# Reordering the opening of a small-attention block: blank products, spare buffers, work moved to GpSimd, loads one a turn

## The chip, the cores and the metric

The kernel runs on one core of a Trainium2 chip. The metric is the device time of one execution in microseconds, as the median of several runs. A core has TensorE (PE in the profile; PEld is its weight load), VectorE (DVE), ScalarE (ACT), GpSimd (POOL) and SyncE (SP, which here only issues DMA transfers). Each engine works through its own list of instructions in order and waits on semaphores for the others.

## What is computed

The reference takes x, 64 sequences of 32 tokens with 256 features in f32, a context of 64 x 257 tokens of 256 features, and a mask. It adds residual blocks, each on a layer norm of x without weights: (1) cross-attention, 16 heads of 16 features, on the first 32 context tokens with a causal window and rotary positions; (2) causal self-attention of the same shape with rotary positions on even and odd features; (3) a linear layer with fp8-quantised weights and activations; (4) cross-attention on all 257 context tokens; (5) a gated mixer with a cumulative sum and a short convolution; (6) a mixture of eight experts, two per token, with one shared. Only the opening of blocks 1 and 2 is touched by the change. Cut to that:

```python
y = (x - mean(x)) / sqrt(var(x) + 1e-5)
q = rope(y @ Wq.T + bq) * d**-0.5        # 16 heads of d = 16
k = rope(ctx[:, :32] @ Wk.T + bk)        # block 2: from y
v = ctx[:, :32] @ Wv.T + bv              # block 2: from y
p = softmax(where(causal, q @ k.T, -inf))
x = x + (p @ v) @ Wo.T + bo
```

## The kernel before

The 2048 tokens stand in SBUF as four tiles `xs[g]` of 512 tokens (128 partitions x 4 x 256). `small_attentions` (L246 to L628) computes blocks 1 and 2 as eight groups n = 0 to 7: n = 0 to 3 are the four token tiles in block 1, n = 4 to 7 the same in block 2. A group has four **turns** t of 128 tokens, called (n,t) below. The Python loops fix the order: every instruction issued through the wrappers (L106 for DVE, ACT, POOL and SP, L118 for products, L121 for transposes) is kept in program order on its engine. So an instruction that waits holds all that follows it on its engine, SP's transfers included.

In turn (n,t) five stages of different tiles run side by side (`line`): the scores of tile t, the sums and the exponentials' transpose of earlier tiles, the context product, the change to feature order, the output product and its addition to x. Beside them the turn prepares group n+1: `rotated` makes one of four rotations (keys c = 0 and 1, then queries c = 0 and 1, in turns 0 to 3), `values` makes v and stores it to DRAM (`v_rows`), `blocks` loads v back in block form (`vb`, whose other places are zeros from a clear at the start), and `spread_keys` copies the keys into block form (`kb`). The layer norm of group n+2 (`norm_steps`, L123 to L182) is a generator stepped by `prepare`: its pieces are the statistics, then mean, variance and three Newton passes for the inverse root, then y in two halves. `opened` transposes y (psT, then ACT copies it to yT).

A rotation is: TensorE product into PSUM (`ps_qk`), DVE's `part` = (product + bias) x sine, four DMA copies `far` that swap blocks of 32 partitions, `near` = (product + bias) x cosine (on DVE for group 0, on ACT and POOL for the others), and the addition near + far on POOL into kT or qT. `near`, `part` and `far` come from rings of two, two and three buffers: a third `near` waits until the first has been added.

The first group's preparation stands ahead of the loop (L500 to L538). The loads are issued by the generator `first_loads` (L632 to L661), stepped by `next(loads)`: before the loop three times, and at the end of turns while n < 3 (in turn 0 the keys' source `kvT` of group n+2 is loaded instead). `raw` (128 x 512 bytes) holds the fp8 weights of block 3; DVE reads it (CAST scratch<-raw) as the first piece of a list of side jobs, in turn (1,0).

Of the kernel before, what the change touches and what calls it, by code (L numbers as in the profile page):

```python
# [7 lines left out]
F32 = mybir.dt.float32  # L8
BF16 = mybir.dt.bfloat16
# [55 lines left out]
def perceiver_kernel(ctx: ExitStack, tc: tile.TileContext, a: dict, out: bass.AP):  # L65
# [54 lines left out]
    def turn(ps, src, eye):  # L120
        return kept(nc.tensor.transpose(ps, src, eye))  # L121

    def norm_steps(g, eng=None, apart=False, ts=range(NT), by_act=False):  # L123

        x = xs[g]
        n, t0 = len(ts), ts[0]
        st = small.tile([P, n, 6], F32, tag="st", name="st")
        mv = small.tile([P, n, 2], F32, tag="mv", name="mv")
        for t in range(n):
            vector.bn_stats(st[:, t, :], x[:, t0 + t, :])  # L130
        if apart:
            yield
        for t in range(n):
            vector.bn_aggr(mv[:, t, :], st[:, t, :])

        ve = small.tile([P, n], F32, tag="ve", name="ve")
        vector.tensor_scalar(ve, mv[:, :, 1], EPS, None, ALU.add)
        half = small.tile([P, n], I32, tag="half", name="half")
        vector.tensor_scalar(half, ve.bitcast(I32), 1, None, ALU.logical_shift_right)
        r0 = small.tile([P, n], I32, tag="r0", name="r0")  # L140
        vector.tensor_scalar(r0, half, -1.0, float(0x5F3759DF), ALU.mult, ALU.add)
        r = r0.bitcast(F32)
        for _ in range(3):
            sq = small.tile([P, n], F32, tag="sq", name="sq", bufs=6)
            rn = small.tile([P, n], F32, tag="rn", name="rn", bufs=6)
            if eng is vector:
                vector.tensor_tensor(sq, r, r, ALU.mult)
                vector.scalar_tensor_tensor(sq, sq, -0.5, ve, ALU.mult, ALU.mult)
                vector.scalar_tensor_tensor(rn, sq, 1.5, r, ALU.add, ALU.mult)
            else:  # L150
                gpsimd.tensor_tensor(sq, r, r, ALU.mult)
                gpsimd.tensor_tensor(sq, sq, ve, ALU.mult)
                gpsimd.tensor_scalar(sq, sq, -0.5, 1.5, ALU.mult, ALU.add)
                gpsimd.tensor_tensor(rn, sq, r, ALU.mult)
            r = rn
        if by_act:
            off = small.tile([P, n], F32, tag="off", name="off")
            gpsimd.tensor_scalar(off, mv[:, :, 0], -1.0, 1.0, ALU.mult, ALU.mult)
            gpsimd.tensor_tensor(off, off, r, ALU.mult)
        yield  # L160
        y = ypool.tile([P, n, D], F32, tag="y", name="y")
        for t in range(n):
            if by_act:
                scalar.activation(
                    y[:, t, :],
                    x[:, t0 + t, :],
                    AF.Identity,
                    bias=off[:, t : t + 1],
                    scale=r[:, t : t + 1],
                )  # L170
            else:
                vector.tensor_scalar(
                    y[:, t, :],
                    x[:, t0 + t, :],
                    mv[:, t, 0:1],
                    r[:, t : t + 1],
                    ALU.subtract,
                    ALU.mult,
                )
            if t == 1 and n > 2:  # L180
                yield
        return y  # L182
# [63 lines left out]
    def small_attentions(layers, first_loads, decode, sides, load_layer1, layer1):  # L246
# [27 lines left out]
            scalar.copy(mk, cst[:, at : at + S][:, None, :].to_broadcast([P, 8, S]))  # L274
            masks.append(mk)

        def clear(vb, engine):
            engine.memset(vb.rearrange("p b h g e -> p (b h g e)"), 0.0)

        def fetch(n):  # L280
            layer, g = order[n]
# [22 lines left out]
        def rotated(it, i, c):  # L304

            src, cs, sn = (
                (it["kvT"], cos, sin) if i == 1 else (it["yT"], cosq, sinq)
            )
            place = "kT" if i == 1 else "qT"
            if c == 0:  # L310
                it[place] = kT_all if i == 1 else qT_([P, 2, GT], "qT")
            dst = it[place]
            w, v0 = it["w"], it["v0"]
            ps = pa([P, GT], "ps_qk")
            proj(ps, lambda k: w[:, i, k, c * P : (c + 1) * P], lambda k: src[:, k, :])

            def by_place(table):
                return table.rearrange("p (o q) -> p o q", o=1).to_broadcast([P, 16, S])

            def by_seq(tile_):  # L320
                return tile_.rearrange("p (b q) -> p b q", q=S)

            bias = vec[:, v0 + 2 * i + c : v0 + 2 * i + c + 1]
            part = part_([P, GT], "part")
            vector.scalar_tensor_tensor(
                by_seq(part), by_seq(ps), bias, by_place(sn), ALU.add, ALU.mult
            )

            far = far_([P, GT], "far")
            for at in range(0, P, S):  # L330
                queue = scalar if (it["n"], i, c) == (0, 0, 1) and at >= 2 * S else sync
                queue.dma_start(out=far[at : at + S, :], in_=part[at ^ S : (at ^ S) + S, :])
            near = near_([P, GT], "near")
            if it["n"] > 0:
                scalar.activation(near, ps, AF.Identity, bias=bias)
                gpsimd.tensor_tensor(by_seq(near), by_seq(near), by_place(cs), ALU.mult)
            else:
                vector.scalar_tensor_tensor(
                    by_seq(near), by_seq(ps), bias, by_place(cs), ALU.add, ALU.mult
                )  # L340
            return lambda: gpsimd.tensor_tensor(dst[:, c, :], near, far, ALU.add)
# [156 lines left out]

        kT_all = sb.tile([P, 2, GT], F32, tag=wide[4], name="kT")
        eye = sb.tile([P, S], BF16, tag="eye", name="eye")  # L500
        loads = first_loads()
        next(loads)
        it = group(0, fetch(0))
        next(loads)
        after = group(1, fetch(1))
        next(loads)
        for half in range(2):
            clear(vbs[0][half], vector)
            clear(vbs[1][half], gpsimd)
        scalar.copy(ident_bf, ident)  # L510
        mask(0)
        it["y"] = finish(norm_steps(order[0][1], vector))
        it["kb"] = [None, None]
        adds = [rotated(it, 1, 0)]
        opened(it)
        mask(1)
        vector.tensor_tensor(eye, ident[:, 0:S], ident[:, 64 : 64 + S], ALU.add)
        steps = norm_steps(order[1][1], vector, apart=True)
        next(steps)
        adds.append(rotated(it, 1, 1))  # L520
        adds[0]()
        for part in range(2):
            spread_keys(it, 0, 0, part)
        adds.append(rotated(it, 0, 0))
        adds.append(rotated(it, 0, 1))
        adds[1]()
        for part in range(2):
            spread_keys(it, 0, 1, part)
# [1 line left out]
            add()  # L530
        for pair in range(2):
            values(it, pair)
        after["y"] = finish(steps)
        for half in range(2):
            blocks(it, half)
        now = it


        line = [None] * 5
        adds = []  # L540
# [1 line left out]
        for n in range(len(order) + 1):  # L542
# [3 lines left out]
                after["kb"] = [None, None]  # L546
            kvT = coming = None
            if n + 2 <= last:
                side = norm_steps(order[n + 2][1], None if n else vector, apart=True)
            else:  # L550
                side = sides

            def prepare(at):
                if n + 2 <= last and at:
                    try:
                        next(side)
                    except StopIteration as end:
                        return end.value

            for t in range(NT):  # L560
                if line[2]:
# [5 lines left out]
                    elif after is not None:  # L567
                        kb_now = (after, 0, t - 2)
                due, adds = adds, []
                if t == 0:  # L570
                    for add in due:
                        add()
                    due = []
# [4 lines left out]
                if after is None:  # L578
                    next(layer1, None)
                else:  # L580
                    y = prepare(t % 2 == 1)
                    adds.append(rotated(after, *((1, 0), (1, 1), (0, 0), (0, 1))[t]))
                if line[3]:
                    by_feature(line[3])
                prepare(t % 2 == 0)
                if n + 2 > last:
                    next(side, None)
                    next(side, None)
# [9 lines left out]
                    next(layer1, None)  # L598
                elif t % 2 == 0:
                    values(after, t // 2)  # L600
                    if (n, t) == (0, 0):
                        opened(after)
                elif t == 3:
                    for half in range(2):
                        blocks(after, half)
                    if n + 2 <= last:
                        coming = group(n + 2, kvT)
                        coming["y"] = y
                        opened(coming)
                line[0] = scores(now, t) if n <= last else None  # L610
                if (n, t) == (last, NT - 1):
                    pair_pool.close()
# [19 lines left out]
    def first_loads():  # L632
# [12 lines left out]
        sync.dma_start(out=xs[1], in_=x_view[1])  # L645
        yield
        sync.dma_start(out=xs[2], in_=x_view[2])
        sync.dma_start(out=w_cur[:, 3], in_=a["w_l0x"][:, 3])
        row_load(R_XO0)
        sync.dma_start(out=xs[3], in_=x_view[3])  # L650
        yield
        sync.dma_start(out=raw, in_=a["w_fp8"])
        for at in (R_AO0, R_FF, R_XO1, R_GO):
            yield
            row_load(at)
        for i in range(0, 4, 2):
# [1382 lines left out]
```

## Time and profile before

| | us |
|---|---|
| median of 3 runs (lowest, highest) | 921.27 (919.26, 922.29) |
| the profiled execution, time | 918.21 |
| its span in the profile | 916.4 |
| PE busy in the span | 853.7 (93%) |
| DVE, POOL, ACT busy | 590.7, 498.1, 424.3 |
| first product of group 0 starts | 7.53 |
| first norm's y complete (DVE) | 10.48 |
| first addition of keys kT (POOL) | 17.86 |
| last addition of queries qT ends (POOL) | 26.08 |
| first scores, (0,0) | 30.24 |
| first scores of (0,1), (0,2), (0,3) | 32.84, 37.56, 44.09 |
| first scores of (1,0), (1,1) | 50.48, 55.14 |

A timeline line is: start, busy time, engine, program line, operation, output<-inputs, shapes, count, and in brackets the idle time of the engine just before and what ended it. Times are in microseconds from the start of the span. L106, L118 and L121 are the wrappers, so a line is found by its tile's name. PE is the product, PEld its weight load beside it. Since POOL and DVE are timed by records of the same profile, rows of one can be set beside the other's by their start times.

### The profile page before, as it was taken

To read this page: it belongs to the slowest core of one execution; us is meant where nothing else is said; L and a number is where in the kernel's file an instruction comes from. 1 tells how busy PE (TensorE), PEld (TensorE's weight loads), DVE (VectorE), ACT (ScalarE), POOL (GpSimd) and SP (SyncE) were. 2 spreads that over 40 slices of the span, in tenths; PEclk is the share of its full clock that TensorE was granted. 3 is DMA by queue.
4 is the path that set the end of the run, shared out by engine and by line. 5 is a ranking of instruction groups with operands and counts; after the bars stand their busy time and mean duration, and the time that the engine had idled before them with its cause. 6 is when DMAs were issued, how large, how long until landed. Compare 5 with 4: busy or idle time off the path is not lost. (4 is left out here: it accounts for less than half of the span.)

```text
span 916.4 us, 22803 instructions
## 1 busy us (share of the span) xinstructions
PE 853.7 (93%) x8699; PEld 587.5 (64%) x8699; DVE 590.7 (64%) x1729; ACT 424.3 (46%) x1100; POOL 498.1 (54%) x982
## 2 busy tenths in 40 slices
PE   6899999989899999999999999998989879999993
PEld 3466666665456666666666666565656648888882
DVE  7888777896677578676777566878655862111117
ACT  2566666653655454554554556654443212222210
POOL 3577777764865566474755566746542124555430
PEclk9999999989999999999999999999799979999997
DMA  7445333453011001111111013000001046777758
GB/s 245 140 135 142 97 90 102 126 154 94 24 53 53 28 28 53 53 54 53 53 53 41 14 53 99 2 2 24 1 25 35 24 155 202 235 231 227 220 181 275
DMA packets 66926, 88.79 MB, mean 97 GB/s; under 512 B 32480, under 2 KB 50688, under 8 KB 64768
## 3 DMA queue, kind: packets, MB, share of 16 engines
q1 hardware_dynamic: 63264, 77.75, 28.2%
q0 software_dynamic: 3456, 9.44, 3.1%
q8 instruction: 69, 1.13, 0.5%
q14 instruction: 41, 0.34, 0.1%
q10 hardware_dynamic: 96, 0.13, 0.1%
HBM read 65.80 MB, written 13.11 MB: 86 GB/s over the span
## 5 line engine op out<-in xcount | busy, mean ns | idle before, releaser
L106 ACT ACTIVATE e<-e,xnm 128x257 f32<-128x257 f32 x256 | 127.2, 499 | 51.2 <-DVE xnm L106 45.7
L106 DVE CUSTOM_DVE_ANT_0 e<-ps_s,mask 128x257 f32<-128x257 f32 x256 | 93.5, 421 | 49.8 <-PE ps_s L118 49.4
L118 PE MATMUL ps_k<-ct,w_w_l1x 128*128 128x512 f32 x256 | 122.3, 600 | 1.6 <-ACT yT L106 0.6
L118 PE MATMUL ps_v<-w_w_l1x,ct 128*128 128x256 f32 x512 | 121.9, 381 | 0.0
L106 POOL TENSOR_SCALAR e<-e,xsm 128x256 f32<-128x256 f32 x256 | 121.3, 492 | 0.0
L121 PE MATMUL ps_t<-cst,e 128*128 128x128 f32 x640 | 102.7, 283 | 7.8 <-DVE eT L106 6.8
L106 DVE COPY eT<-ps_t 128x512 f32<-128x512 f32 x128 | 88.0, 687 | 28.5 <-PE ps_t L121 28.1
L118 PEld LDWEIGHTS ps_v<-w_w_l1x,ct 128*128 128x128 f32 x512 | 94.1, 192 | 11.1 <-issue 0.2
L106 POOL TENSOR_TENSOR x<-x,rows 128x256 f32<-128x256 f32 x96 | 70.8, 753 | 41.9 <-ACT y L106 16.9
L106 ACT ACTIVATE kT<-ps_k,vec 128x512 f32<-128x512 f32 x64 | 44.0, 688 | 100.7 <-PE ps_k L118 100.4
L121 PEld LDWEIGHTS ps_t<-cst,e 128*128 128x128 f32 x640 | 71.9, 142 | 26.3 <-DVE eT L106 7.6
L106 ACT ACTIVATE hTr<-ps_h,w 128x256 f32<-128x256 f32 (+1 forms) x80 | 31.3, 450 | 115.3 <-issue 88.9
L106 DVE TENSOR_TENSOR og<-ps_o,b 128x512 f32<-128x512 f32 (+1 forms) x20 | 12.8, 638 | 104.5 <-PE ps_o L118 104.5
L118 PEld LDWEIGHTS ps_k<-ct,w_w_l1x 128*128 128x128 f32 x256 | 44.5, 190 | 41.3 <-issue 35.3
L1802 POOL DMA_INDIRECT r_rows<-og,lv x36 | 35.5, 986 | 61.3 <-DVE og L106 56.4
L118 PE MATMUL ps_h<-ygT,w 128*128 128x256 f32 (+1 forms) x320 | 65.8, 359 | 0.6 <-issue 0.6
L118 PE MATMUL ps_o<-w,hTr 128*128 128x256 f32 x288 | 65.3, 379 | 0.0
L106 ACT COPY v<-ps_v 128x512 f32<-128x512 f32 x80 | 46.4, 581 | 38.6 <-PE ps_v L118 38.5
L106 POOL TENSOR_TENSOR last<-e,xsm 128x4 f32<-128x4 f32 x64 | 12.9, 202 | 88.9 <-DVE xsm L106 88.9
L118 PEld LDWEIGHTS ps_h<-ygT,w 128*128 128x128 f32 x320 | 54.9, 190 | 6.6 <-issue 0.8
L118 PEld LDWEIGHTS ps_o<-w,hTr 128*128 128x128 f32 x288 | 54.4, 190 | 7.2
L106 ACT ACTIVATE kb<-kT,cst 128x256 f32<-128x256 f32 x96 | 45.4, 512 | 27.2 <-POOL kT L106 25.4
(207 smaller groups left out, 1655.9 us busy)
## 6 DMA issues: line engine op xcount, KB each, us to landing
ct<-in_ctxT SPq DMA_DIRECT2D x16, 1024.0 KB
w<-in_ew SPq DMA_DIRECT2D x20, 514.0 KB
w<-in_ew SPq DMA_DIRECT2D x20, 512.0 KB
far<-part SPq DMA_DIRECT2D x126, 64.0 KB
v_rows<-v SPq DMA_DIRECT2D x16, 256.0 KB
vb<-v_rows SPq DMA_DIRECT2D x64, 64.0 KB
r<-r_rows SPq DMA_DIRECT2D x8, 512.0 KB
b<-in_eb SPq DMA_DIRECT2D x20, 128.0 KB
```

What stands on the lines that cost most here:

```text
L106: ins = getattr(self.engine, name)(*args, **kw)
L118: return kept(nc.tensor.matmul(ps, **args))
L121: return kept(nc.tensor.transpose(ps, src, eye))
L1802: wrote = nc.gpsimd.indirect_dma_start(out=r_rows, out_offset=bass.IndirectOffsetOnAxis(ap=write_i[:, at : at + 1], axis=0), in_=o[:, i, : ...
```

## The change

In the order of the diff:

1. `norm_steps` can stop once more (`split`) ahead of the Newton passes. Group 1's norm uses it: statistics, mean and variance stand before the keys' additions, the Newton passes after the queries' products.
2. All four clears of `vb` (128 x 2048 f32 each) are on GpSimd; before, two were on DVE.
3. Both rotations of group 0's keys are issued ahead of the transposes of y.
4. Their `part` and `near` take buffers of the scores' rings (tags sc0, sc1, e0, e1), which hold nothing until the first scores; the queries' come from the two rings as before.
5. DVE clears a bf16 tile `blank`, and TensorE multiplies it by itself 14 times (128x512 each) into PSUM bank b5 ahead of all else. Nothing reads the result.
6. Group 2's norm: its Newton passes run on GpSimd instead of DVE, and its pieces move: statistics in turn (0,1), mean, variance and Newton passes in (0,2), all of y in (0,3). Before, the four pieces came one a turn from (0,0) to (0,3).
7. In all turns of group 0 the additions near + far left by the turn before come first; before, they came first in turn 0 only, and in the others after the feature-order stage.
8. `opened` of group 1 moves from the end of turn (0,0) to that of (0,1). Group 0's eight block loads move from before the loop into turns (0,0) and (0,1), four each.
9. `first_loads` has one more stop: x2 is issued once the values of group 0 are made, w_l0x[3] and a rows load in turn (0,1), x3 in (0,2), raw and another rows load in (0,3), and the rest a turn or more later than before. Before, x2, w_l0x[3], rows and x3 were issued at the start and raw in (0,1).

```diff
-    def norm_steps(g, eng=None, apart=False, ts=range(NT), by_act=False):
+    def norm_steps(g, eng=None, apart=False, ts=range(NT), by_act=False, split=False):
...
         r = r0.bitcast(F32)
+        if split:
+            yield
         for _ in range(3):
...
-        def clear(vb, engine):
-            engine.memset(vb.rearrange("p b h g e -> p (b h g e)"), 0.0)
+        def clear(vb):
+            gpsimd.memset(vb.rearrange("p b h g e -> p (b h g e)"), 0.0)
...
-            part = part_([P, GT], "part")
+            spare = (it["n"], i) == (0, 1)
+            part = sb.tile([P, GT], F32, tag=f"sc{c}", name="part") if spare else part_([P, GT], "part")
...
-            near = near_([P, GT], "near")
+            near = sb.tile([P, GT], F32, tag=f"e{c}", name="near") if spare else near_([P, GT], "near")
...
+        blank = sb.tile([P, GT], BF16, tag="e2", name="blank")
+        vector.memset(blank, 0.0)
+        idle = psum.tile([P, GT], F32, tag="b5", name="idle")
+        for _ in range(14):
+            mm(idle, lhsT=blank[:, 0:P], rhs=blank, start=True, stop=True)
         loads = first_loads()
         next(loads)
         it = group(0, fetch(0))
         next(loads)
         after = group(1, fetch(1))
-        next(loads)
-        for half in range(2):
-            clear(vbs[0][half], vector)
-            clear(vbs[1][half], gpsimd)
+        for vb in vbs[0] + vbs[1]:
+            clear(vb)
...
-        adds = [rotated(it, 1, 0)]
+        adds = [rotated(it, 1, c) for c in range(2)]
         opened(it)
...
-        steps = norm_steps(order[1][1], vector, apart=True)
+        steps = norm_steps(order[1][1], vector, apart=True, split=True)
         next(steps)
-        adds.append(rotated(it, 1, 1))
+        next(steps)
         adds[0]()
         for part in range(2):
             spread_keys(it, 0, 0, part)
         adds.append(rotated(it, 0, 0))
         adds.append(rotated(it, 0, 1))
+        next(steps)
         adds[1]()
...
         for pair in range(2):
             values(it, pair)
+        next(loads)
         after["y"] = finish(steps)
-        for half in range(2):
-            blocks(it, half)
...
-                side = norm_steps(order[n + 2][1], None if n else vector, apart=True)
+                side = norm_steps(order[n + 2][1], apart=True)
...
+            ahead, behind = ((0, 1, 0, 1), (1, 0, 1, 0)) if n else ((0, 0, 1, 2), (0, 1, 0, 0))
...
-                if t == 0:
+                if t == 0 or n == 0:
                     for add in due:
                         add()
...
-                    y = prepare(t % 2 == 1)
+                    y = prepare(ahead[t])
...
-                prepare(t % 2 == 0)
+                prepare(behind[t])
...
-                    if (n, t) == (0, 0):
-                        opened(after)
+                elif (n, t) == (0, 1):
+                    opened(after)
...
+                if n == 0 and t < 2:
+                    blocks(now, t)
                 line[0] = scores(now, t) if n <= last else None
...
         sync.dma_start(out=xs[2], in_=x_view[2])
+        yield
         sync.dma_start(out=w_cur[:, 3], in_=a["w_l0x"][:, 3])
         row_load(R_XO0)
+        yield
         sync.dma_start(out=xs[3], in_=x_view[3])
         yield
         sync.dma_start(out=raw, in_=a["w_fp8"])
-        for at in (R_AO0, R_FF, R_XO1, R_GO):
+        row_load(R_AO0)
+        for at in (R_FF, R_XO1, R_GO):
             yield
             row_load(at)
```

More of the change, by code (lines that the diff above doesn't have):

```diff
@@ L548, in small_attentions, with prepare @@
             if n + 2 <= last:
-                side = norm_steps(order[n + 2][1], None if n else vector, apart=True)
+                side = norm_steps(order[n + 2][1], apart=True)
             else:
                 side = sides
-            def prepare(at):
-                if n + 2 <= last and at:
+            def prepare(count):
+                y = None
+                for _ in range(count if n + 2 <= last else 0):
                     try:
@@ L557, in prepare @@
                     except StopIteration as end:
-                        return end.value
+                        y = end.value
+                return y
+            ahead, behind = ((0, 1, 0, 1), (1, 0, 1, 0)) if n else ((0, 0, 1, 2), (0, 1, 0, 0))
             for t in range(NT):
```

## The prediction

> **What bounds the kernel now.** I read the table of busy time in ten-microsecond windows first, then the timelines of the engines from 7 to 58 us (the change ends where the second group begins), then the issues on SP's queue. In the windows the columns are engine busy time (PE, PEld, DVE, ACT, POOL), the granted clock, the DMA share and GB/s:
>
> ```profile
> 0.00:10.00 10.00, 2.47 (x3) 1.17 (x4) 7.94 (x25) 1.89 (x3) 3.73 (x6) 1.00 0.78 269
> 10.00:20.00 10.00, 8.89 (x30) 4.73 (x28) 6.31 (x14) 2.22 (x6) 2.04 (x3) 1.00 0.77 250
> 20.00:30.00 10.00, 6.86 (x27) 4.36 (x28) 9.14 (x27) 4.22 (x11) 4.69 (x6) 1.00 0.52 141
> 30.00:40.00 10.00, 9.69 (x180) 5.99 (x179) 8.46 (x28) 5.91 (x13) 4.44 (x5) 1.00 0.52 149
> 40.00:50.00 10.00, 9.06 (x107) 5.82 (x106) 8.35 (x18) 8.14 (x18) 7.45 (x8) 1.00 0.43 116
> 50.00:60.00 10.00, 9.35 (x173) 6.11 (x172) 9.03 (x24) 6.48 (x16) 6.10 (x17) 1.00 0.66 183
> 60.00:70.00 10.00, 10.00 (x184) 7.34 (x183) 7.89 (x15) 6.55 (x16) 7.91 (x10) 1.00 0.34 95
> ```
>
> From 60 us on TensorE has no idle time. What the opening gains or loses for TensorE by then stays to the end; there are some 14 us of idle TensorE before 60 us, 7.5 of them before the first product. From 50 us on DVE has no gap either, and its order is fixed by the program:
>
> ```profile
> 48.64 0.75 DVE L106 SCALAR_TENSOR_TENSOR part<-ps_qk,vec,cst 128x512 f32<-128x512 f32 x1 [0.77 <-PE ps_qk L118]
> 49.31 1.39 DVE L106 BATCH_NORM_STATS2 st<-x 128x6 f32<-128x256 f32 x4
> 50.62 1.22 DVE L106 CAST scratch<-raw 128x512 int32<-128x512 int8 x1
> 51.77 0.68 DVE L106 TENSOR_REDUCE mx<-pair_bank 128x16 f32<-128x512 f32 x1
> ```
>
> The cast at 50.62 starts with nothing ahead of it to wait for, because its load was issued at 38.53 and landed at 42.30. Everything behind it runs back to back until 57.6 at least.
>
> **The opening, part by part.** (Turn (n,t) is turn t of group n; part and far are the rotation's product and its partition-swapped copy.)
>
> Clears. DVE loses two clears of 1.77 us, the second ending at 5.14; the statistics of x0 (5.06) then start when x0 is there (4.65), so the first norm ends at 10.17 instead of 10.48. GpSimd gets four at 1.80: 0.73 to about 7.9, so the clears stand beside the small Newton operations that begin at 6.7. What a clear does to a DVE operation on two SBUF inputs no row shows: DVE's and GpSimd's clears overlap without slowing (1.77 and 1.80), and against a GpSimd addition DVE's small operations are blocked for as long as the addition lasts:
>
> ```profile
> 23.65 1.23 DVE L106 SCALAR_TENSOR_TENSOR rn<-sq,rn 128x4 f32<-128x4 f32 x1
> 24.91 1.19 DVE L106 TENSOR_TENSOR sq<-rn 128x4 f32<-128x4 f32 x1
> ```
>
> (0.16 alone.) So the price lies between 0 and one clear's rest, 1.2 to 1.4: y of x0 ends between 10.2 and 11.5. I take half. [...]
>
> Blank products. The first key product took 3.37 us, the second 1.95; the granted clock reads 1.00 at both, so that column doesn't show what made the first slow. One blank costs between 0.27 (a bf16 128x256 row, warm) and 0.84 (a quarter of the 3.37, which is four records): 14 of them 3.8 to 11.8 us, in idle time until 7.5. I take 0.27 x 1.73 = 0.47 each, 6.5, ending at 8.0. Then k0 is ready at 8.0 + 1.95 = 9.95, hidden by y's end in place of 10.94. If they don't warm anything, k0 is at 11.4 and k1 at 14.7; if each takes 0.84, they end at 13 and the opening loses 2: the two ends. [...]
>
> Keys first, spare buffers. Before, part k0 is at 10.94 and part k1 at 14.49 (behind transposes), the near of q0 waits for the kT addition (19.16) and that of q1 too (20.98). After, k0 at 10.2 and k1 at about 11.5; the queries no longer wait for the ring. A rotation costs 0.75 for part, 2.42 to issue its four copies, 1.4 to land. With the bulk loads out of the way, kT0 is added at 15.0 (17.86), kT1 at 17.5 (19.68), the queries' copies land at 21.2 (24.20) and the last query addition ends at 22.6 (26.09). With the block of 1.3 each is 1.3 later. So the first scores come at 23.6 to 25, against 30.24. The second norm's Newton is issued after the queries' products; it is free of their near waits but meets the additions, at one blocked operation (1.2) each. The first key product of group 1 (before: 28.08) starts its rotation at 22.9 to 25.9; I take 25.0, **3.1 earlier**.
>
> **The turns of group 0.** Here that gain is spent. Group 2's norm (x2) ran on DVE: 33.46 to 35.2 for Newton. Now it runs on GpSimd, as x3's does in before: 12 operations from 55.64 to 58.93, 3.3 us, issued behind the addition of kT11, which waits for far11. TensorE's transposes of y stand before scores (0,3), so they wait for it. From the start of the first rotation of group 1: part 0.75, copies 2.5, one v_rows store 0.45, four block loads now moved into turn 0 at 0.49 = 1.95, the kvT load 0.45, copies of far11 2.5, landing 1.45: 10.05. Then kT11 1.27, the spread 0.5, Newton 3.3, y 1.4: 16.5; with 0.25 of hand-overs 16.75. DVE's y is delayed by up to two GpSimd additions that follow (near and qT): 0, 1.25 or 2.5. So q1's part of group 1 starts 16.75 to 19.25 after the first; before:
>
> ```profile
> 28.08 0.75 DVE L106 SCALAR_TENSOR_TENSOR part<-ps_qk,vec,cst 128x512 f32<-128x512 f32 x1
> ...
> 42.31 1.25 DVE L106 TENSOR_SCALAR y<-x,mv,rn 128x256 f32<-128x256 f32 x2
> 43.48 0.74 DVE L106 SCALAR_TENSOR_TENSOR part<-ps_qk,vec,cst 128x512 f32<-128x512 f32 x1
> ```
>
> 15.4 after. With 25.0 + 18.2 = 43.2 the gain is **0.3 us** of 3.1 (ends: 22.9 + 16.75 = 39.7, a gain of 3.8, and 25.9 + 19.25 = 45.2, a loss of 1.7). TensorE, given the first scores five us earlier, waits in turn (0,3) instead. Sums first costs nothing: the additions that it moves ahead are waited for by the keys' spread behind them anyway. x2, w3, rows and x3 land late but ahead of use: x2 is wanted at about 30, and is issued at about 22.
>
> **The raw load.** It moves from the end of turn (0,1) to the end of (0,3). On SP it then stands behind the last rotation's copies and the eight block loads:
>
> ```profile
> 42.88 0.49 SPq L106 DMA_DIRECT2D rows<-in_rows  x1
> 44.29 2.42 SPq L106 DMA_DIRECT2D far<-part  x4
> 46.75 4.86 SPq L106 DMA_DIRECT2D vb<-v_rows  x8
> 51.66 0.45 SPq L106 DMA_DIRECT2D rows<-in_rows  x1
> ```
>
> Its place is that of the last line: 51.66 less 0.3. From the end of the q1 part: copies 2.45, blocks 3.9 (at 0.49) to 4.86, own issue 0.5 to 0.6, landing 1.45 (a far copy) to 3.2 (this load before; the rows load above took 2.73, to 54.84): 8.3 to 11.1. The cast comes 6.4 after that end. DVE stalls **1.9 to 4.7, I take the middle, 3.3**, and nothing takes that up: mx of (1,0), which stands behind the cast, waits, then the part of group 2's first query, then the chain to ACT's cT, for which TensorE waits already:
>
> ```profile
> 57.71 1.13 PE L118 MATMUL ps_p<-w_w_l0x,cT 128*128 128x256 f32 x4 [0.65 <-ACT cT L106]
> ```
>
> **Sum.** -0.3 + 3.3 = 3.0 us later for TensorE at 60 us, and so at the end. The profiled execution took 918.21 us (span 916.4 and 1.8 around it), so it would take 921.2; the median of the runs, 921.27, stands 3.06 above that execution, so I forecast **924.3**. The ends: a gain of 3.8 with a stall of 1.9 gives -1.9, 919.4; a loss of 1.7 with 4.7 gives +6.4, 927.7.
>
> **Rivals.**
> - *The opening's gain reaches the end (faster).* Place: the x2 chain. If far11 isn't held by SP's queue (the block loads issued in the shade of other waits) and GpSimd's Newton is done before y is wanted, scores (0,3) come when TensorE's own work allows: from first scores at 24 and the 13.85 between (0,0) and (0,3) in before, 37.9 against 44.09, 6.2 earlier. With the smaller stall, 1.9, that leaves 4.3: 917.0. It decides from the point at which the q1 part comes before 40. For it: 14 us of idle TensorE to take. Against: the sum of 16.75, each term from a row.
> - *Gain and stall cancel.* The raw load lands like a far copy (stall 1.9) and the opening keeps some 2 us: 921.3. For: the load is 64 KB (128x512 of one byte), no more than one far copy. Against: it took 3.19 in before.
> - [...] Clears block the first norm (1.3), GpSimd's additions block y twice (2.5): q1 part at 45.2, stall 4, +5.7: 927.0. For: the rows of 1.23 and 1.19. Against: before had such blocks in the second norm too.
> - *The blanks don't warm.* Then k1 comes at 14.7 as before, 1.3 more: inside the forecast's range.
>
> **How the numbers follow.** Forecast 0.55 (own range 919.4 to 927.7), gain reaches the end 0.24, cancel 0.09, lock twice 0.12. About 0.3% (2.76 us) is what a measurement of this kernel can tell from no change. Of the forecast's 0.55 some 0.36 lies above +2.76 and 0.19 within it. So slower 0.36 + 0.12 = 0.48, same 0.19 + 0.09 = 0.28, faster 0.24. The range takes in half of the first rival below and the lock's end above: 916.5 to 928.5.
>
> **What would show it.** First scores at 23.6 to 25; Newton of x1 with one or two entries of 1.2; the first key part of group 1 at 23 to 26; GpSimd's x2 Newton directly behind kT11; the psT of group 2 waiting for y; the raw load on SP behind the eight block loads, and ahead of the cast an idle time of 2 to 5 us put down to the DMA of raw. It would be wrong if the q1 part came before 40, or the cast did not wait, or if TensorE had idle time after 60 us that took up a delay.

## The result and the profile after

The changed kernel takes **925.57 us** (median of 8 runs, 924.02 to 928.49); the kernel before took 920.88 beside it (8 runs, 918.99 to 922.29). The ratio is 1.0058, interval 1.0043 to 1.0074: slower by 4.0 to 6.8 us. Its profiled execution took 925.07 us, span 923.3 (before: 918.21 and 916.4).

Windows of the changed kernel (columns as in the prediction):

```profile
0.00:10.00 10.00, 8.04 (x19) 3.00 (x20) 5.25 (x21) 1.89 (x3) 7.22 (x8) 1.00 0.78 265
...
20.00:30.00 10.00, 9.68 (x115) 6.08 (x113) 9.52 (x21) 6.55 (x15) 4.74 (x5) 1.00 0.58 170
30.00:40.00 10.00, 7.55 (x95) 4.53 (x94) 6.80 (x17) 6.30 (x13) 5.44 (x9) 1.00 0.71 183
40.00:50.00 10.00, 5.50 (x89) 4.13 (x90) 6.07 (x9) 3.47 (x8) 5.83 (x12) 0.66 0.49 143
```

TensorE works 2.8 us more from 20 to 30 us than before, and 5.7 us less from 30 to 50 us. Of its 8.04 us in the first ten, 5.96 go to the blank products, which nobody reads.

The opening did what it was meant to do: the first scores start at 24.69 us instead of 30.24. Half of the lead is gone at the third tile, and all of it at the fourth. First scores of each turn, from the timelines of TensorE:

| turn | before | after | difference |
|---|---|---|---|
| (0,0) | 30.24 | 24.69 | -5.55 |
| (0,1) | 32.84 | 28.70 | -4.14 |
| (0,2) | 37.56 | 35.01 | -2.55 |
| (0,3) | 44.09 | 46.63 | +2.54 |
| (1,0) | 50.48 | 53.53 | +3.05 |
| (1,1) | 55.14 | 58.92 | +3.78 |
| (1,2) | 62.44 | 67.43 | +4.99 |
| (2,0) | 74.36 | 79.36 | +5.00 |

Two places turn the lead into a loss: ahead of (0,3), where 5.1 us go, and between (1,0) and (1,2), where 1.9 go. From there to (2,0) the difference stays at 5.0. Of the 3.0 us lost from (0,0) to (0,2), 1.4 come with the transposes of group 1's y, which the change moved behind the first scores, and 1.33 are a wait for yT at 31.37.

**The first place.** GpSimd of the changed kernel, from the addition of the second keys' rotation of group 1:

```profile
37.21 1.27 POOL L106 TENSOR_TENSOR kT<-near,far 128x512 f32<-128x512 f32 x1 [3.99 <-DMA far<-part]
38.46 0.48 POOL L106 TENSOR_SCALAR kb<-kT,cst 128x256 f32<-128x256 f32 x1
38.90 0.21 POOL L106 TENSOR_TENSOR sq<-r 128x4 f32<-128x4 f32 x1
...
41.99 0.20 POOL L106 TENSOR_TENSOR rn<-sq,rn 128x4 f32<-128x4 f32 x1
42.14 1.26 POOL L106 TENSOR_TENSOR near<-near,cst 128x512 f32<-128x512 f32 x1
43.48 1.26 POOL L106 TENSOR_TENSOR qT<-near,far 128x512 f32<-128x512 f32 x1
```

and DVE, which waits for the last Newton operation and then stands through GpSimd's two large operations:

```profile
42.23 3.48 DVE L106 TENSOR_SCALAR y<-x,mv,rn 128x256 f32<-128x256 f32 x4 [3.71 <-POOL rn L106]
45.62 0.74 DVE L106 SCALAR_TENSOR_TENSOR part<-ps_qk,vec,cst 128x512 f32<-128x512 f32 x1
```

Undisturbed, the four operations of y take 1.38 (a row of the kernel before, from group 1's norm):

```profile
26.79 1.38 DVE L106 TENSOR_SCALAR y<-x,mv,rn 128x256 f32<-128x256 f32 x4
```

Here they take 3.48. TensorE meanwhile:

```profile
38.50 0.38 PE L121 MATMUL ps_c<-cst,o 128*128 128x128 f32 x2
43.70 0.44 PE L121 MATMUL psT<-cst,y 128*128 128x128 f32 x1 [4.82 <-DVE y L106]
44.95 1.76 PE L121 MATMUL psT<-cst,y 128*128 128x128 f32 x7 [0.81 <-DVE y L106]
46.63 0.41 PE L118 MATMUL pair_bank<-mk,eye 64*32 64x256 bf16 x8
46.82 1.08 PE L118 MATMUL pair_bank<-kb,qT 64*32 64x128 f32 x32
```

and in the kernel before:

```profile
43.39 0.78 PE L121 MATMUL psT<-cst,y 128*128 128x128 f32 x4 [0.94 <-DVE y L106]
44.09 0.30 PE L118 MATMUL pair_bank<-mk,eye 64*32 64x256 bf16 x8
44.22 0.64 PE L118 MATMUL pair_bank<-kb,qT 64*32 64x128 f32 x32
```

A second cost stands behind the wait of 4.82. The granted clock, 0.66 as the mean of the ten microseconds, is 1.00 until 40.97, 0.50 from there to 47.79 (the last 2.7 of the wait and the work behind it) and 1.00 again from then on; at 0.50 the 32 score products take 1.08 instead of 0.64.

**The second place.** SP's queue, and DVE at the cast:

```profile
46.42 2.41 SPq L106 DMA_DIRECT2D far<-part  x4
48.90 5.39 SPq L106 DMA_DIRECT2D vb<-v_rows  x8
54.33 0.45 SPq L106 DMA_DIRECT2D raw<-in_w_fp  x1
```

```profile
52.36 1.40 DVE L106 BATCH_NORM_STATS2 st<-x 128x6 f32<-128x256 f32 x4
56.41 0.43 DVE L106 CAST scratch<-raw 128x512 int32<-128x512 int8 x1 [2.65 <-DMA raw<-in_w_fp]
56.76 0.68 DVE L106 TENSOR_REDUCE mx<-pair_bank 128x16 f32<-128x512 f32 x1
```

The raw load stands behind the block loads, the cast waits 2.65 us for it, and everything behind the cast waits with it. TensorE meets this as a wait for cT, 1.66 long; before, the same wait was 0.65, at 57.71:

```profile
62.71 1.13 PE L118 MATMUL ps_p<-w_w_l0x,cT 128*128 128x256 f32 x4 [1.66 <-ACT cT L106]
```

### The profile page after: what moved, and what is told of

Read it like the earlier page. It is cut to its first block, busy times and chain, and to the rows that moved or that the text cites. A ratio compares the mean times of both kernels' runs of the same rounds, so it can differ in the third digit from the quotient of the medians.

```text
span 923.3 us, 22828 instructions
## 1 busy us (share of the span) xinstructions
PE 858.3 (93%) x8713; PEld 588.8 (64%) x8713; DVE 588.7 (64%) x1719; ACT 424.5 (46%) x1100; POOL 503.4 (55%) x996
## 5 line engine op out<-in xcount | busy, mean ns | idle before, releaser
L106 POOL TENSOR_TENSOR x<-x,rows 128x256 f32<-128x256 f32 x96 | 70.7, 752 | 45.2 <-ACT y L106 19.0
L106 POOL DMA_INDIRECT yg<-y_rows,lv x36 | 35.1, 975 | 39.7 <-DVE lv L106 29.1
```

Of the source, the lines that this page charges most:

```text
L106: ins = getattr(self.engine, name)(*args, **kw)
```

## The experiments

The theory: the cost is those two places, the Newton passes on GpSimd and the late raw load; the other parts gain or do nothing. The main rivals: one of the two is hidden behind the other; or the opening's gain is lost in group 0 whatever is done. In the table, "first scores (2,0)" is from each kernel's profile, against 74.36 in the kernel before; ratios are to the kernel before.

| kernel | median us | before beside it | ratio (95%) | first scores (2,0) |
|---|---|---|---|---|
| changed | 925.57 | 920.88 | 1.0058 (1.0043 to 1.0074) | +5.00 |
| raw early | 924.68 | 920.69 | 1.0044 (1.0029 to 1.0058) | +4.33 |
| norm 2 put back | 927.67 | 920.69 | 1.0075 (1.0058 to 1.0092) | +8.19 |
| both | 922.77 | 920.69 | 1.0021 (1.0009 to 1.0033) | +2.52 |
| before, raw late | 924.07 | 920.69 | 1.0029 (1.0017 to 1.0042) | +3.92 |
| norm 2's Newton on DVE | 922.15 | 920.63 | 1.0007 (0.9992 to 1.0022) | +2.49 |
| two clears on DVE | 925.67 | 920.63 | 1.0056 (1.0040 to 1.0072) | +6.19 |
| no blank products | 926.20 | 920.63 | 1.0060 (1.0038 to 1.0082) | +4.81 |
| three parts undone | 919.59 | 920.63 | 0.9981 (0.9966 to 0.9996) | -0.94 |
| the same, y in halves | 920.68 | 920.61 | 0.9996 (0.9980 to 1.0013) | -0.73 |
| before, opening alone | 919.46 | 920.61 | 0.9982 (0.9970 to 0.9994) | -1.29 |
| the same, with blanks | 918.58 | 919.95 | 0.9981 (0.9966 to 0.9996) | -1.72 |
| the same, with the turns | 918.74 | 919.95 | 0.9981 (0.9967 to 0.9995) | -1.65 |

The last column and the medians go together to about 1.2 us: the time is decided by then.

**Raw early.**

```diff
         sync.dma_start(out=xs[2], in_=x_view[2])
+        sync.dma_start(out=raw, in_=a["w_fp8"])
         yield
...
-        sync.dma_start(out=raw, in_=a["w_fp8"])
         row_load(R_AO0)
```

> The changed kernel, with the load of raw issued directly behind x2's (about 23 us) instead of at the end of turn (0,3). In the changed kernel the cast waits 2.65 us for it (56.41) and TensorE meets that again in a wait of 1.66 us for cT at 62.71. Theory (two separate losses, the late norm of group 2 and the late raw load): the cast starts at about 53.8, the output product at 62.71 comes 2.2 earlier, and the time falls from 925.6 to 923.3. Rival (the late norm alone sets the end, the cast's wait stands beside it): no idle time ahead of the cast, but 925.6 as before.

The cast has no idle time any more (54.68, right behind the statistics); the time falls by 0.9, not 2.3, and the intervals of the two ratios overlap. In the profiled execution the first query products took 5.40 us instead of 3.70, so first scores came 1.7 later for a reason that is not in the edit; but that execution, 922.54, was the fastest of the six, so this does not explain the median. Between (1,0) and (1,2) this kernel takes 12.23, the changed one 13.90, the kernel before 11.96: the second place is closed. By the medians alone the theory's size isn't shown here.

**Norm 2 put back, alone and with raw early.**

```diff
-                side = norm_steps(order[n + 2][1], apart=True)
+                side = norm_steps(order[n + 2][1], None if n else vector, apart=True)
...
-            ahead, behind = ((0, 1, 0, 1), (1, 0, 1, 0)) if n else ((0, 0, 1, 2), (0, 1, 0, 0))
+            ahead, behind = (0, 1, 0, 1), (1, 0, 1, 0)
```

> The changed kernel, with group 2's norm as in the kernel before: Newton passes on DVE, one piece a turn from (0,0) to (0,3). Theory: TensorE's wait of 4.82 us for y ahead of scores (0,3) goes, scores (0,3) come at 40 to 42 instead of 46.63 and TensorE is 4 to 5 us earlier from there; the raw load still stands behind the eight block loads, so the cast still waits 2 to 4 us: 920.5 to 921.5. Rival (the chain is that of the rotations' copies and additions, not the norm): scores (0,3) within 1 us of 46.6 and 925.

> The changed kernel with both edits: raw issued behind x2's load, and group 2's norm as in the kernel before. Theory (the two losses add up, and the opening's gain is real): 925.6 - 2.2 - 4.5 = 918.9, some 2 us below the kernel before (920.9), with the cast not waiting and scores (0,3) at 40 to 42. Rival (the opening's gain is taken away by something else, the block loads or the sums first): 920.9 or above.

Alone it gains nothing (927.67 against 925.57, with intervals that overlap), and the expectation failed: scores (0,3) came at 46.93. With both edits the 918.9 that was expected failed too, and 922.77 is the rival's side. The wait for y at (0,3) is gone, but another has come ahead of it. TensorE with both edits:

```profile
30.30 0.66 PE L121 MATMUL ps_t<-cst,e 128*128 128x128 f32 x4
36.90 3.75 PE L118 MATMUL ps_qk<-yT,w_w_l0x 128*128 128x512 f32 x4 [5.94 <-ACT yT L106]
```

In the kernel before, Newton ran on DVE in turn (0,1), ahead of the rotation of that turn, while the transposes of group 1 were already done. The change has moved those transposes into (0,1): ACT's yT copies stand behind the near of that turn's rotation (34.41), which waits for DVE's part (33.56), which stands behind Newton. The four query products behind the wait take 3.75 us instead of 1.88; the granted clock is 0.68 as the mean of 30 to 40 us, and 1.00 there in the kernel before. So the place of the norm's pieces had to change with the transposes; the engine was free, as the run with Newton on DVE below shows. With the norm put back, the raw load counts in full: the two kernels differ in that load alone, and by 4.9 us.

**Before, raw late.**

```diff
-        sync.dma_start(out=raw, in_=a["w_fp8"])
         for at in (R_AO0, R_FF, R_XO1, R_GO):
             yield
+            if at == R_FF:
+                sync.dma_start(out=raw, in_=a["w_fp8"])
             row_load(at)
```

> The kernel before, with one edit: the load of raw issued at the end of turn (0,3), where the changed kernel has it (behind the eight block loads), all else as it was. Theory (the late load alone costs its wait): issue at about 51.7, landing 53.7 to 54.5, so the cast waits 2.3 to 3.2 us, less the 0.8 by which it is shorter when no GpSimd operation blocks it: 922.5 to 923.5 against 920.9. Rival (TensorE has enough queued work to hide it): 920.9.

The load is issued at 53.08 behind 5.66 us of block loads, the cast waits 4.00, and the kernel before becomes 3.4 us slower (2.7 by the ratio, interval 1.6 to 3.9). One late 64 KB load is enough. In its profile 0.64 of the 3.92 us at (2,0) stand already at (1,0), ahead of the cast, so some 3.3 are the load's. The rival falls: TensorE had no queued work to hide it.

**Norm 2's Newton on DVE, at the changed place.** The first line of the diff above alone.

> The changed kernel with group 2's Newton passes on DVE, all pieces of that norm at the places where the changed kernel has them (Newton in turn (0,2), y in (0,3)). In the changed kernel y waits for GpSimd's last Newton operation at 41.99 and is blocked there for 2.1 us (42.23 to 45.71); TensorE waits 4.82 for it, at a clock that falls to 0.66. Theory (the engine of the Newton passes is what costs, because on GpSimd they stand behind the addition that waits for the copies): y starts at 39 to 40, scores (0,3) come at 42 to 43.5 instead of 46.63, the raw load still costs its wait: 922 to 923. Rival (the place of the pieces in the turns costs, not the engine): within 1 us of 925.6, as the norm put back whole gained nothing (927.7).

Scores (0,3) come at 42.75, and 3.4 us of the loss are back with one argument, as the theory said; the rival falls. What is left is the cast, which now waits longer, since the rest is earlier:

```profile
39.82 2.40 DVE L106 TENSOR_SCALAR y<-x,mv,rn 128x256 f32<-128x256 f32 x4
...
53.67 0.66 DVE L106 CAST scratch<-raw 128x512 int32<-128x512 int8 x1 [3.99 <-DMA raw<-in_w_fp]
```

This is the first rival of the theory in part: a repair of one place gives the other more to hide.

**Two clears on DVE.**

```diff
-        for vb in vbs[0] + vbs[1]:
-            clear(vb)
+        for half in range(2):
+            clear(vbs[0][half], vector)
+            clear(vbs[1][half], gpsimd)
```

> The changed kernel with two of the four clears on DVE again. In the changed kernel DVE's first small operation behind the mean took 1.50 us (6.30) instead of 0.17 and ended when the fourth GpSimd clear did. Theory: that operation takes 0.17, y of x0 is complete at 10.0 instead of 11.3, all of the opening comes 1.0 to 1.3 earlier, scores (0,0) at 23.5, and the time falls by 1 to 1.3: 924.4. Rival (what waits later for copies and loads swallows it): scores (0,0) earlier, scores (0,3) and the time within 0.5 of the changed kernel.

In the changed kernel DVE is held by a clear; GpSimd's clears last from 0.74 to 7.78:

```profile
5.90 0.36 DVE L106 BATCH_NORM_AGGREGATE mv<-st 128x2 f32<-128x6 f32 x4
6.30 1.50 DVE L106 TENSOR_SCALAR ve<-mv 128x4 f32<-128x4 f32 x1
```

The statistics (1.41) and the mean (0.36) run beside the clear; the tensor-scalar operation, the next of its kind taking 0.17, ends with it, at 7.80. With two clears on DVE it takes 0.17 and y ends 0.64 earlier. At the first scores 0.5 is left, because the second norm's y now meets GpSimd's query additions (21.49, 3.54 us); at (0,3) nothing is left (46.83), and the time is the same. The rival held.

**No blank products.** The loop runs 0 times instead of 14.

> The changed kernel without the 14 blank products (the clear of their tile stays). In the changed kernel the two key products took 3.67 together; the kernel before took 3.37 for its first alone. Theory (blanks bring the products to full speed): first key product 3.4, the second 1.9 to 3.4, the keys' second rotation at 13.3 to 14.7 instead of 12.63, scores (0,0) 0.7 to 2 later and the time up by as much: 926.5 to 927.5. Rival (waits later in group 0 swallow it): scores (0,3) and the time within 0.5 of the changed kernel.

Without them the two key products together:

```profile
6.83 5.56 PE L118 MATMUL ps_qk<-kvT,w_w_l0x 128*128 128x512 f32 x8 [6.83 <-DMA kvT<-in_ctx32T]
```

and with them, in the changed kernel:

```profile
1.19 5.96 PE L118 MATMUL idle<-blank 128*128 128x512 bf16 x14 [1.19 <-DVE blank L106]
7.92 3.67 PE L118 MATMUL ps_qk<-kvT,w_w_l0x 128*128 128x512 f32 x8 [0.77 <-DMA kvT<-in_ctx32T]
```

Behind the blanks the two take 1.9 us less, 3.67 instead of 5.56. The first record of the granted clock, 1.00, comes at 6.83 in the trace of the changed kernel, ahead of its key products, and at 10.38 in that of the kernel before, where the first key product takes 3.37 from 7.53 on. The 1.00 that the windows show ahead of these times stands on no record, which is why the prediction read 1.00 at a slow product. But the load of the keys' source came a microsecond earlier in the run without, the second key part waits for DVE as well, and the first scores are at 24.69 in both. The times can't be told apart: the rival held.

**Three parts undone.** Newton on DVE, raw early and two clears on DVE together, the diffs as above.

> The changed kernel with three parts undone: Newton of group 2 on DVE (at the changed place), raw issued behind x2's load, two clears on DVE. What stays: blank products, keys first, spare buffers, sums first, the other loads one a turn. Theory (these three are the cost, and the rest gains): scores (0,0) at 23.5, (0,3) at 41 to 42.5, no wait of the cast, TensorE 2 to 3 us ahead of the kernel before from there: 918 to 919. Rival (the opening's gain is lost in group 0 whatever is done, as the run with the norm put back whole suggests): 920.9 or more.

919.59, faster than the kernel before. Alone, the three give 3.4, 0.9 and nothing (by medians); together 6.0. Raw early gave 0.9 alone and 4.9 with the norm put back, so what one part gives depends on the others. Newton and raw undone with all four clears on GpSimd wasn't run, so what the clears give in that company isn't shown. Of the lead of 6.2 us at the first scores 2.4 are left at (0,3) and 0.6 at (1,1). TensorE now waits at (1,0) for the addition of the last query rotation:

```profile
48.23 0.40 PE L118 MATMUL pair_bank<-kb,qT 64*32 64x128 f32 x16
50.20 0.45 PE L118 MATMUL pair_bank<-kb,qT 64*32 64x128 f32 x16 [1.57 <-POOL qT L106]
```

**The same, y in halves.** The tables for group 0 are (0, 0, 1, 1) and (0, 1, 1, 0).

> The changed kernel with the same three parts undone as in the run before this (Newton of group 2 on DVE in turn (0,2), raw with x2, two clears on DVE), and group 2's y in two halves again, one in (0,2) and one in (0,3). In that run all of y stood at 38.77 to 41.19 ahead of the last query rotation of group 1 (41.11), and TensorE waited 1.30 for y there and 1.57 for that rotation's addition at 50.20. Theory (y ahead of the rotation sets that addition): the rotation starts 0.7 to 1.2 earlier, scores (0,3) at 40.5 to 41, 918.5 against 919.6. Rival (DVE has no gap in turn (0,2) either): 919.6.

The last rotation starts at 41.38 instead of 41.11, and the time is that of the kernel before. In this profile, too, the query products took 5.40 instead of 3.70, which puts all of it 1.7 later at the first scores; (0,3) is 0.3 later. Most of the 1.7 is made up at (0,1) already (29.21 against 28.59), ahead of the halves, so no gain of theirs is shown.

**Before, opening alone.** The kernel before with parts 1, 3 and 4 of the change: both key rotations first, spare buffers, the split of the second norm.

> The kernel before with three parts of the change alone: both key rotations ahead of the transposes, their spare buffers, and the second norm's Newton passes behind the queries' products. No blank products, loads, clears, norms and turns as before. Theory (these parts are the opening's gain, and group 0 in the order of before passes it on): first scores at 26 to 28 instead of 30.24, as the bulk loads still slow the copies, scores (0,3) at 41 to 43, no wait of the cast, 917.5 to 919.5. Rival (the gain comes from the deferred loads, or group 0 swallows it): 920.6.

919.46. First scores at 28.43, later than expected since they still stand behind the transposes of group 1, but (0,3) at 42.81, and the 1.3 us are kept to (2,0). The last query addition ends at about 24.2 instead of 26.08: with both rotations first and the queries no longer waiting for the ring. The loads deferred by the change aren't needed for it. At (0,1) only 0.32 of the 1.81 us of lead is left: the 32 score products take 1.08 us instead of 0.64 and the four key products behind them 2.96 instead of 1.98, and the granted clock is 0.91 from 20 to 30 us and 0.92 from 30 to 40 (1.00 in both in the kernel before).

**With blanks, and with the turns.** Both add the 14 blank products to that kernel. The second also moves the transposes of group 1 to (0,1) and group 2's norm as in the change, on DVE.

> The kernel before with both key rotations ahead, spare buffers and the split of the second norm (as in the run that measured 919.46 against 920.61), and the 14 blank products. There the two key products took 5.68 us, with blanks 3.67 in the changed kernel. Theory (the blanks' 2 us reach only what waits for the keys' second product; DVE is behind y until 11.9 anyway): second key part 1 to 1.5 earlier, scores (0,3) 0.3 to 1 earlier, 918.6 to 919.2. Rival (as in the changed kernel without blanks, the copies of the next waits swallow it): 919.5.

> The same kernel as the one with the blanks beside it, and the turns of the change: the transposes of group 1's y in turn (0,1), group 2's norm with Newton in (0,2) and all of y in (0,3), on DVE. Loads, clears and the order of additions as before. Theory (first scores no longer stand behind those transposes, and the loads' early issue costs the copies 1 to 2 us): scores (0,0) at 25 to 26.5, (0,3) at 41 to 42, 918.5 to 919.5, the same as the kernel beside it. Rival (the early loads are what costs, and only their deferral makes the turns pay): 920 or more.

918.58 and 918.74, the same ratio of 0.9981; without blanks it was 0.9982, so the blanks show no gain here either. First scores come at 28.24 in the one and 25.39 in the other, and at (0,3) it is 42.32 and 42.56: three microseconds earlier at the first tile are worth nothing at the fourth. The second kernel differs from the one with three parts undone only in when loads and blocks are issued (raw, too) and in sums first, and both have 0.9981: no gain or loss of those parts can be measured within the intervals of 0.15%.

## Why the prediction was right

The forecast was 924.3 (+3.0), the result 925.57 (+4.7). The direction, both places and both waits were right; the sizes were not, and their errors partly cancel. By the rows, the -0.3 of the norm's chain was +2.1, the clock, which the sum didn't have, added some 0.9, and the +3.3 of the raw load reached TensorE as 1.9: together 5.0 at (2,0). That the number came as close as it did is in part luck.

- **The opening** came as worked out. First scores at 24.69 (23.6 to 25 was said), the first key rotation of group 1 at 25.28 (25.0 taken), the block by the clears at 1.33, the upper of the two ends of 0 to 1.4. It is the row of 1.50 instead of 0.17, though the operation held is a tensor-scalar one and not, as the prediction had it, one with two SBUF inputs. The blanks took 5.96 here and 4.79 to 6.09 in the other nine profiles with blanks; 6.5 was taken. The 10.17 of the first norm's end is 10.07 by the prediction's own figures (10.48 less 5.06 - 4.65); nothing rests on the 0.1.
- **The chain through x2's norm** was the right one, and it was the mis-sized term. "16.75 to 19.25", with 18.2 taken, measured 25.28 to 45.62 = 20.34, so the predicted gain of 0.3 is a loss of 2.1. Two terms were short: the last of far11's copies landed at 36.91, 2.50 after its issue instead of 1.45, with the 512 KB kvT load in flight until 35.90 (4.02 to land; that it is the cause is argued, not shown); and SP's issues began 0.6 later than their sum. Newton took the 3.3 that were said, and GpSimd's two operations delayed y by 2.1, within the 0 to 2.5.
- **The raw load** was right in place and mechanism: behind the eight block loads, a wait of 2.65 against 3.3 taken. With the rest as before it is 4.00, within the 1.9 to 4.7. The sum missed that the late cast is shorter, 0.43 instead of 1.22 (before, GpSimd's near ran beside it, from 50.28 to 51.56): 2.65 less 0.79 is the 1.9 that TensorE loses between (1,0) and (1,2).
- **What the sum left out**: TensorE's clock, 0.50 until 47.79. An estimate from the rows: first scores of (0,3) start 1.01 behind q1's part instead of 0.61, and (1,0) follows 6.90 later instead of 6.39, some 0.9 in all.
- **The rival of the clears and additions that block DVE** came true in its parts: the first norm was 1.33 later beside the clears (1.3 was said), y took 2.1 longer beside GpSimd's two operations (2.5), and q1's part came at 45.62 (45.2). Only its stall of 4 was too long. It had 0.12, and its +5.7 is nearer to the measured +4.7 than the forecast's +3.0 is.
- **The rival of the gain that reaches the end** was priced with its condition, the last query part before 40. No kernel here met it: the best came to 41.1, and kept 1.0 us.
- **TensorE without idle time from 60 us on** holds for the windows shown, not for the kernel: busy 853.7 of a span of 916.4, it has some 49 us of idle time behind them. It took up little all the same, +5.0 at (2,0) against +4.7 at the end. DVE's run without a gap ends at 59.3 (1.29 idle ahead of 60.60).

What stays open: why first scores 1.8 to 6.2 us earlier end in 1.0 to 1.4 in all four faster versions. The waits for yT (1.33), y (1.30) and the last query addition (1.57) in the version with three parts undone name where it goes; none was taken away by itself. In two of the four, the opening alone and with blanks, 1.5 and 1.6 of it go by (0,1), where the key products of group 1 behind the first scores take 2.96 and 3.58 instead of 1.98; at (0,3) the lead is 1.28 and 1.77 again.

## What to carry to other kernels

In this kernel a late load cost what is queued behind its reader: before a load is moved, count what stands ahead of it on its queue at the new place, and what stands behind the waiting instruction. A small chain moved to an idle engine inherits that engine's queue: twelve operations of 0.2 us cost several microseconds because an addition that waits for copies stood ahead, and two large operations that block the reader (3.48 instead of 1.38) stood behind. Time won at the first tile counts only as far as the next wait in order; test parts both alone and together, since two losses can hide each other.

## What the runs showed of the hardware

- A DVE tensor-scalar operation on 128x4 elements was held for the whole rest of a GpSimd clear (1.50 against 0.17), while statistics and mean on DVE beside the same clears took 1.41 and 0.36 (1.34 and 0.36 in the kernel before).
- The speed of TensorE differed from run to run with the same order of work: group 0's query products, behind a wait of some 0.7, took 3.70 in seven of the ten profiles with blanks and 5.40 in three (raw early, norm 2's Newton on DVE, y in halves); the granted clock from 10 to 20 us was 1.00 in the seven and 0.83 in the three. What set the three apart isn't shown.
- In the changed kernel the granted clock went from 1.00 to 0.50 at 40.97, 2.1 us into TensorE's wait of 4.82 for y, and back to 1.00 at 47.79, 4.1 us after that wait's end; TensorE was busy for 3.29 of the 6.82 us between. What sets these two times isn't shown.
- The eight block loads at the end of turn (0,3) took SP 4.86 us to issue in the kernel before, 5.39 in the changed kernel and 5.66 in the kernel before with raw late, so 0.61 to 0.71 each. Group 0's took 3.78 as eight in the kernel before, and 2.02 and 2.11 as four each in the changed kernel. So a queue's price at one place was no constant.
